# Ninth layer's attention in three-place steps with a written-out engine order, and the last layers' attention values by column strips

## The chip, the cores and the metric

The kernel runs on one core of one Trainium2 chip. The metric is the device time of one execution in microseconds (us); each kernel's time is the median of several runs. Engine names as the profile has them: PE (TensorE, matmuls), PEld (its weight loads), DVE (VectorE), ACT (ScalarE), POOL (GpSimd), SP (SyncE, which issues the transfers).

## The reference, cut to what matters

Twelve layers, four blocks of cross attention, attention and feed-forward, each added to `x` after a layer norm. `x` is 128 x 32 x 128 (batch, sequence, channels), all in float32. The change touches the ninth layer and the eleventh.

```
# ninth layer (L2_ffn): T, B, C = 128, 32, 128; H = 16 heads of D = 8
x0 = layernorm(x)
q, k, v = split(x0 @ in_proj_w.T + in_proj_b)             # attention runs over the 128 batch entries
attn = softmax(einsum('tbhd,sbhd->bhts', q, k) / sqrt(D))  # for each of 32 places b and 16 heads: 128 x 128
ctx  = einsum('bhts,sbhd->tbhd', attn, v)
h = layernorm(x0 + ctx @ out_w.T + out_b, ln1_g, ln1_b)
logits = h @ router_w.T + router_b                         # the router picks one of 8 experts, gelu, layernorm
# eleventh layer (L3_attn): 128 sequences of 32, 16 heads of 8
scores = einsum('bhqd,bhkd->bhqk', q, k) * scale + rel_bias
out = einsum('bhqk,bhkd->bhqd', softmax(scores), v) @ W_out.T + b_out
```

## The kernel before, in words

`x` lives on chip as eight tiles `X[g]` (128 rows x 4 x 128). The layers run one after the other, each in stages over groups; a tile framework puts each engine's instructions in an order at compile time, by the order in which the program writes them and by what they wait for. Tiles come from pools with a fixed number of buffers, and a new tile waits until the old user of its buffer is done. `issue_after(i)` keeps what is written inside it behind instruction `i` on its engine.

**Ninth layer, `L2_ffn`.** `x` goes through DRAM so that a row becomes a batch entry: `XB[q]`, eight groups `q` of four places. For a group: `stats` (DVE, with a power on POOL for the inverse root, L214), `normed` to `xn`, four transposes `pxt` copied by ACT to `xT`, projections `pq`, `pk`, `pv` to `QT`, `KT`, `V` by DVE. Then `L2_ffn_place` for each of the four places, and `end(q-1)`: second layer norm, transposes `pht`, `HT` (ACT), router `plg`, `LG` (DVE).

A place has two halves. `L2_ffn_scores`: POOL makes `KM` (the keys masked by head, L248); four score matmuls, one for each strip of 32 rows, fill four banks `S` (L1388, L1391; one buffer each); for each bank DVE takes the negated maximum `nm` (L1398, L1396) and ACT makes four exps with their sums `sm` (L1401). `L2_ffn_values`: sixteen transposes into banks `pt` of two buffers (L1412), copied to `ET` by DVE (L1417), the fourth by ACT (L1415); four matmuls `pav`, one for each strip of 32 output partitions (L1419, L1423); reciprocal of `sm` (L1424), spread by POOL to `rb` (L1426), transposed to `pr` (L1429), copied by ACT to `Rs` (L1431); DVE forms `O` = `pav` x `Rs` (L1433). `L2_ffn_out`: four matmuls `pw` (L1441), added to `xn` by DVE (L1442). All of `pxt`, `pq`, `pk`, `pv`, `pht`, `plg`, `pav`, `pr`, `pw` share a PSUM pool `bpq` of two buffers.

`L2_ffn_place` writes the scores of place n first, then the output of place n-2 and the values of place n-1, and orders PE alone: scores behind the `pr` of the values written before them, the rest behind the scores. Group work is written between the places, all of a group at once:

```
                    for i in range(4):
                        self.L2_ffn_place(QT[:, i, :], KT[:, i, :], V[:, i, :], xn[:, i, :], WO, st, ba, bps, bpt, bpq)
                    ends.append(lambda q=q, xn=xn: end(q, xn))
                    if q:
                        ends.pop(0)()
```

**Last layers, `L3`.** For each of eight groups the tenth layer (`xattn13`), the eleventh (`L3_attn`) and, one group later, the twelfth (`L3_ffn`) are interleaved by `abreast`. `L3_attn` works on 4 sets of four sequences per group, 32 in all: scores `S` of 32 x 32 blocks (L1528), bias and maximum (DVE), exp (ACT), 32 x 32 transposes on DVE to `ET`, values spread to `Vb` by POOL (L620). Then 16 value matmuls `po` (L1543) in two halves of eight heads, all with outputs on partitions 0 to 31; for each half a reciprocal (L1545) and a multiplication to `O` (L1546); four transposes `pot` (L1550), `OT` copied by ACT (L1552), one projection matmul `pw` (L1554), added to `X` by DVE (L1555). `po`, `pot` and `pw` share two buffers of `lpo`.

Of the kernel before, what the change touches and what calls it, by code (L numbers as in the profile page):

```python
# [9 lines left out]
FP = mybir.dt.float32  # L10
I32 = mybir.dt.int32
U32 = mybir.dt.uint32
AF = mybir.ActivationFunctionType
# [26 lines left out]
def _kxm(a):  # L40

    return np.ascontiguousarray(a.T)


def _blocks(d):
# [61 lines left out]
    f["L3_attn"] = [("wqkv", _kxm(g(p + "W_qkv"))), ("wo", _kxm(g(p + "W_out"))), ("bo", _rep(g(p + "b_out"))),  # L107
# [57 lines left out]
class Kern:  # L165
# [1099 lines left out]
    def L2_ffn(self, w):  # L1265
# [8 lines left out]
        with self.pool("bx") as bx:  # L1274
# [8 lines left out]
            with self.pool("bw") as bw, self.pool("bs", 2) as bs, self.pool("ba", 2) as ba, self.pool("bps", 1, PSUM) as bps, \  # L1283
# [3 lines left out]
                def end(q, xn):  # L1287
                    mv, rs = self.stats(bs, xn, 4, 1e-5)
                    h = Hn[q]
                    for i in range(4):  # L1290
                        nc.vector.tensor_scalar(h[:, i, :], xn[:, i, :], mv[:, i, 0:1], rs[:, i:i + 1], ALU.subtract, ALU.mult)
                    ps = bpq.tile([128, 512], FP, tag="q", name="pht")
# [3 lines left out]
                    nc.gpsimd.tensor_tensor(h, h, rep("b1n"), ALU.add)  # L1296
                    ps = bpq.tile([128, 4, 8], FP, tag="q", name="plg")
# [3 lines left out]
                st, ends = {}, []  # L1301
                for q in range(NG):
                    mv, rs = self.stats(bs, XB[q], 4, 1e-5)
                    xn = self.normed(bs, XB[q], mv, rs)
                    ps = bpq.tile([128, 512], FP, tag="q", name="pxt")
                    self.transposed(ps, xn)
                    nc.gpsimd.tensor_tensor(xn, xn, rep("bo"), ALU.add)
                    xT = bs.tile([128, 512], FP, tag="xT")
                    nc.scalar.copy(xT, ps)
                    QT = bs.tile([128, 4, 128], FP, tag="QT")  # L1310
                    ps = bpq.tile([128, 4, 128], FP, tag="q", name="pq")
                    nc.tensor.matmul(ps, lhsT=w["wi"][:, 0:128], rhs=xT, start=True, stop=True)
                    nc.vector.tensor_scalar(QT, ps, w["bqk"][:, 0:1], HD ** -0.5, ALU.add, ALU.mult)
                    KT = bs.tile([128, 4, 128], FP, tag="KT")
                    ps = bpq.tile([128, 4, 128], FP, tag="q", name="pk")
                    nc.tensor.matmul(ps, lhsT=w["wi"][:, 128:256], rhs=xT, start=True, stop=True)
                    nc.vector.tensor_scalar(KT, ps, w["bqk"][:, 1:2], None, ALU.add)
                    V = bs.tile([128, 4, 128], FP, tag="V")
                    ps = bpq.tile([128, 4, 128], FP, tag="q", name="pv")
                    for i in range(4):  # L1320
                        nc.tensor.matmul(ps[:, i, :], lhsT=xT[:, i * 128:(i + 1) * 128], rhs=w["wi"][:, 256:384], start=True, stop=True)
                    nc.vector.tensor_tensor(V, ps, rep("bv"), ALU.add)
                    for i in range(4):
                        self.L2_ffn_place(QT[:, i, :], KT[:, i, :], V[:, i, :], xn[:, i, :], WO, st, ba, bps, bpt, bpq)
                    ends.append(lambda q=q, xn=xn: end(q, xn))
                    if q:
                        ends.pop(0)()
                self.L2_ffn_place(None, None, None, None, WO, st, ba, bps, bpt, bpq)
                ends.pop(0)()
# [27 lines left out]
    def L2_ffn_place(self, qT, kT, v, acc, WO, st, ba, bps, bpt, bpq):  # L1357

        tc = self.tc
        last = None  # L1360
        if qT is not None:
            if "pr" in st:
                with tc.issue_after(st["pr"].ins):
                    E, sm, last = self.L2_ffn_scores(qT, kT, ba, bps)
            else:
                E, sm, last = self.L2_ffn_scores(qT, kT, ba, bps)
        with tc.issue_after(last.ins) if last is not None else ExitStack():
            if "out" in st:
                self.L2_ffn_out(*st.pop("out"), WO, bpq)
            if "val" in st:  # L1370
                Ep, smp, vp, accp = st.pop("val")
                O, st["pr"] = self.L2_ffn_values(Ep, smp, vp, ba, bpt, bpq)
                st["out"] = O, accp
        if qT is not None:
            st["val"] = E, sm, v, acc
        else:
            self.L2_ffn_out(*st.pop("out"), WO, bpq)

    def L2_ffn_scores(self, qT, kT, ba, bps):
# [3 lines left out]
        KM = ba.tile([128, 4, 128], FP, tag="KM")  # L1383
        self.masked4(nc.gpsimd, KM, kT)
        E = ba.tile([128, H, 128], FP, tag="E")
        sm = ba.tile([128, H], FP, tag="sm")
        S = [bps.tile([128, 4, 128], FP, tag=f"s{j}", name="S") for j in range(4)]
        last = nc.tensor.matmul(S[3], lhsT=qT[96:128], rhs=KM[96:128], start=True, stop=True)  # L1388
        with self.tc.issue_after(last.ins):
            for j in range(3):  # L1390
                last = nc.tensor.matmul(S[j], lhsT=qT[32 * j:32 * j + 32], rhs=KM[32 * j:32 * j + 32], start=True, stop=True)  # L1391
# [226 lines left out]
```

## Time and profile before

| | |
|---|---|
| median of 3 runs | 5587.87 us (5586.97 to 5591.53) |
| the profiled execution's own time | 5588.02 us |
| its span, first to last instruction | 5586.2 us |
| mean granted PE clock | 0.893 |
| busy: PE, PEld, DVE, ACT, POOL | 4724.7, 3187.2, 3465.5, 2210.5, 1084.1 us |

The profile is of one execution. Busy time is a share over the whole span; the stages have different limits, so the stage is read by its own window, and in it by what each engine waited for. The granted clock is full (1.0) or half (0.5) at any moment, and a window's figure is the mean. A matmul in float32 counts as two entries on PE, a transpose as one.

### The profile page before, as it was taken

What the parts mean: (1) busy time and instruction counts of PE and PEld (TensorE: products, weight loads), DVE (VectorE), ACT (ScalarE), POOL (GpSimd) and SP (SyncE); (2) the same over time, 40 slices, a digit from 0 to 9 for tenths busy, and PEclk for the clock granted to TensorE, in tenths of its full rate; (3) what the DMA queues carried; (4) which work ended last, traced back from release to release, by engine and by line L of the source; (5) the groups of instructions that cost most, each with busy time, mean ns of one, the idle gap of its engine ahead of it and who ended that gap; (6) DMA issues with size and microseconds to landing.
All of it is one profiled execution on the core that took longest, in us unless ns stands there. A gap on an engine that the chain in (4) does not pass through costs nothing. (4 is left out here: it accounts for less than half of the span.)

```text
span 5586.2 us, 89363 instructions
## 1 busy us (share of the span) xinstructions
PE 4724.7 (85%) x34462; PEld 3187.2 (57%) x34462; DVE 3465.5 (62%) x9687; ACT 2210.5 (40%) x5844; POOL 1084.1 (19%) x1065
## 2 busy tenths in 40 slices
PE   8999989898889988898995888888988856668677
PEld 5666656666566656666772555555555533336445
DVE  4333359743884389639724788888788745456554
ACT  3333334333333333355331444454445525453233
POOL 0010102020111111111000222223222221212443
PEclk9999999998899989898995899999999967779777
DMA  3111131123012311231100000100010010000100
GB/s 97 39 43 38 43 57 43 43 58 57 29 40 55 68 34 43 81 56 52 20 5 17 25 20 28 31 26 22 27 29 24 26 38 1 1 1 10 35 12 11
DMA packets 335131, 192.95 MB, mean 35 GB/s; under 512 B 160865, under 2 KB 317281, under 8 KB 334065
## 3 DMA queue, kind: packets, MB, share of 16 engines
q1 hardware_dynamic: 334706, 187.24, 12.7%
q8 instruction: 272, 4.46, 0.3%
q14 instruction: 153, 1.25, 0.1%
HBM read 156.23 MB, written 30.96 MB: 34 GB/s over the span
## 5 line engine op out<-in xcount | busy, mean ns | idle before, releaser
L494 PE MATMUL S<-cT,t 128*128 128x257 f32 x2048 | 552.0, 401 | 65.1 <-ACT E L498 64.3
L214 POOL TENSOR_TENSOR rs<-ve,w_const 128x4 f32<-128x4 f32 (+1 forms) x192 | 193.0, 1006 | 1810.6 <-DVE ve L212 1738.9
L494 PEld LDWEIGHTS S<-cT,t 128*128 128x128 f32 x2048 | 366.6, 194 | 192.0 <-ACT E L498 111.4
L496 DVE TENSOR_REDUCE nm<-S 128x1 f32<-128x257 f32 x512 | 214.7, 421 | 406.1 <-PE S L494 403.5
L498 ACT ACTIVATE E<-S,nm 128x257 f32<-128x257 f32 x512 | 243.4, 476 | 385.1 <-DVE nm L497 380.2
L760 DVE SCALAR_TENSOR_TENSOR X<-py,R,X 128x128 f32<-128x128 f32 x768 | 221.9, 342 | 251.6 <-PE py L753 161.9
L1092 PE MATMUL S<-cT,QM 128*128 128x289 f32 x1024 | 355.9, 445 | 22.5 <-ACT E L1094 20.4
L1094 ACT ACTIVATE E<-S,nm 128x289 f32<-128x289 f32 x512 | 254.9, 501 | 204.2 <-DVE nm L1093 201.7
L518 PE MATMUL po<-TA,cN 128*128 128x512 f32 x512 | 308.3, 690 | 13.0 <-ACT TA L513 12.6
L1101 PE MATMUL pt<-w_const,E 128*96 128x128 f32 (+1 forms) x1536 | 275.3, 291 | 45.7 <-ACT E L1094 38.3
L1101 PEld LDWEIGHTS pt<-w_const,E 128*96 128x96 f32 (+1 forms) x1536 | 190.3, 149 | 183.5 <-ACT E L1094 77.8
L520 ACT COPY OT<-po 128x512 f32<-128x512 f32 x256 | 150.0, 586 | 348.9 <-PE po L519 348.8
L519 PE MATMUL po<-TB,cN 128*128 128x512 f32 x512 | 284.1, 641 | 0.0
L753 PEld LDWEIGHTS py<-w_L_ffn,Hh 128*128 128x128 f32 x2048 | 251.2, 195 | 53.1 <-issue 32.7
L481 ACT COPY t<-pq 128x512 f32<-128x512 f32 x256 | 149.3, 586 | 325.7 <-PE pq L480 325.4
L480 PE MATMUL pq<-xT,WQK 128*128 128x128 f32 x2048 | 251.5, 279 | 27.4 <-DVE xn L220 16.6
L749 ACT ACTIVATE Hh<-pu,w_L_ffn 128x512 f32<-128x512 f32 x256 | 173.4, 687 | 228.7 <-PE pu L748 215.8
L753 PE MATMUL py<-w_L_ffn,Hh 128*128 128x128 f32 x2048 | 259.1, 280 | 3.7 <-ACT Hh L749 3.5
L480 PEld LDWEIGHTS pq<-xT,WQK 128*128 128x128 f32 x2048 | 238.9, 191 | 38.2 <-DVE xn L220 22.1
L1093 DVE TENSOR_REDUCE nm<-S 128x1 f32<-128x289 f32 x512 | 223.4, 449 | 57.2 <-PE S L1092 51.7
L748 PE MATMUL pu<-xT,w_L_ffn 128*128 128x512 f32 x512 | 250.4, 611 | 0.8 <-ACT Hh L749 0.8
L651 DVE TENSOR_TENSOR elt<-A,row 128x544 f32<-128x544 f32 (+23 forms) x304 | 246.8, 812 | 3.4
(477 smaller groups left out, 10775.0 us busy)
## 6 DMA issues: line engine op xcount, KB each, us to landing
cT<-ctxT SPq DMA_DIRECT2D x128, 257.0 KB
cN<-ctx SPq DMA_DIRECT2D x128, 256.0 KB
cT<-ctxT SPq DMA_DIRECT2D x32, 514.0 KB
phik<-PW SPq DMA_DIRECT2D x32, 256.0 KB
phiq<-P SPq DMA_DIRECT2D x32, 256.0 KB
A<-phik SPq DMA_DIRECT2D x64, 128.0 KB
PQ<-phiq SPq DMA_DIRECT2D x32, 256.0 KB
cN<-ctx SPq DMA_DIRECT2D x32, 194.0 KB
```

What stands on the lines that cost most here:

```text
L480: nc.tensor.matmul(ps[:, k, :, :], lhsT=WQK[:, 4 * j + k, cb * 128:(cb + 1) * 128], rhs=xt, start=True, stop=True)
L494: nc.tensor.matmul(S, lhsT=QP[j][:, cb, b, :, :], rhs=cTs[b][:, cb, :], start=cb == 0, stop=cb == 1)
L498: nc.scalar.activation(E[:, j, 0:LK], S, AF.Exp, bias=m, accum_out=sm[:, j:j + 1])
L518: nc.tensor.matmul(po, lhsT=cNs[b][:, 0, c], rhs=TA, start=True, stop=False)
L519: nc.tensor.matmul(po, lhsT=cNs[b][:, 1, c], rhs=TB, start=False, stop=True)
L651: nc.vector.tensor_tensor(t, A[:, k, :, i0:i1].rearrange("p h i -> p i h").unsqueeze(3).to_broadcast([128, m, HC, n]), row[:, :, i0:N].uns ...
L748: nc.tensor.matmul(ps, lhsT=wu[:, e, k * 128:(k + 1) * 128], rhs=xT[:, q, :], start=True, stop=True)
L753: nc.tensor.matmul(py[:, i, :], lhsT=Hh[:, k, i * 128:(i + 1) * 128], rhs=wd[:, e, k, :], start=k == 0, stop=k == 3)
L1092: nc.tensor.matmul(S, lhsT=QM[:, 0, 4 * j:4 * j + 4, :], rhs=cT[:, b, :], start=True, stop=True)
L1093: nc.vector.tensor_reduce(nm[:, j:j + 1], S, AX.X, ALU.max, negate=True)
L1094: nc.scalar.activation(E[:, j, :], S, AF.Exp, bias=nm[:, j:j + 1], accum_out=sm[:, j, b:b + 1])
L1101: nc.tensor.transpose(pt[0:n, j * 128:(j + 1) * 128], E[:, j, k0:k1], self.ident)
```

## The change

In `L2_ffn` the function `L2_ffn_step(n, ...)` takes the place of `L2_ffn_place`, `_scores`, `_values` and `_out`. A step works on three places: scores of n, values of n-1, output of n-2. Helper `follow` chains each listed instruction behind the one listed before it on its engine, so that PE, DVE and ACT each have the order of the text; POOL's work and the group's work on DVE and ACT are not chained. The first three of a place's four transpose banks are made in its own step, the fourth in the next; ACT now copies the third bank, DVE the others. The group's work becomes two generators, `front(q)` and `end(q)`, of which a step takes one piece each; their PE instructions are chained in at that point. Keys are projected ahead of queries, `xn` has three buffers, `sm` three.

In `L3_attn` the value matmuls put head `4j+k` on output partitions 32j to 32j+31, in one bank; one reciprocal and one multiplication follow; four transposes have 128 input partitions and 32 output partitions, ACT copies 32 x 512 for 128 x 128, and the projection is four matmuls over 32 rows each, with `wo` laid out as 32 x 512.

```diff
-    f["L3_attn"] = [("wqkv", _kxm(g(p + "W_qkv"))), ("wo", _kxm(g(p + "W_out"))), ("bo", _rep(g(p + "b_out"))),
+    f["L3_attn"] = [("wqkv", _kxm(g(p + "W_qkv"))), ("bo", _rep(g(p + "b_out"))),
+                    ("wo", g(p + "W_out").T.reshape(4, 32, 128).transpose(1, 0, 2).reshape(32, -1)),
...
+                def front(q):
+                    mv, rs = self.stats(bs, XB[q], 4, 1e-5)
...
+                    nc.scalar.copy(xT, ps)
+                    yield 1
...
+                    nc.vector.tensor_scalar(KT, ps, w["bqk"][:, 1:2], None, ALU.add)
...
+                    nc.vector.tensor_scalar(QT, ps, w["bqk"][:, 0:1], HD ** -0.5, ALU.add, ALU.mult)
+                    yield 1
...
+                    nc.vector.tensor_tensor(V, ps, rep("bv"), ALU.add)
+                    P[q] = QT, KT, V, xn
+                    yield 1
+                def end(q):
+                    xn = P.pop(q)[3]
                     mv, rs = self.stats(bs, xn, 4, 1e-5)
...
+                    yield 1
                     ps = bpq.tile([128, 512], FP, tag="q", name="pht")
...
+                    yield 1
                     ps = bpq.tile([128, 4, 8], FP, tag="q", name="plg")
...
+                for n in range(T + 2):
+                    q, i = n // 4, n % 4
...
+                    if i == 0 and q + 1 < NG:
+                        new = front(q + 1)
+                    old = end(q - 1) if i == 1 and q else old
+                    self.L2_ffn_step(n, pl, ((new,), (new, old), (new, old), (old,))[i], WO, st, ba, bps, bpt, bpq)
...
+    def queue(self, st, *insts):
+        for i in insts:
+            if i.engine in st:
+                self.tc.add_manual_dep(i, st[i.engine].name, mybir.DependencyInfo(mybir.DependencyClass.NoSync, mybir.DependencyReason.DATA),
+                                       reason="issue_after")
+            st[i.engine] = i
...
+    def L2_ffn_step(self, n, pl, side, WO, st, ba, bps, bpt, bpq):
...
+        a, b = st.get(n - 2), st.get(n - 1)
+        if a:
+            a["Rs"] = ba.tile([128, 4, 128], FP, tag="Rs", name="Rs")
+            f(nc.scalar.copy(a["Rs"], a["R"]))
+        if pl is not None:
...
+            for j in (3, 0, 1, 2):
+                r = slice(32 * j, 32 * j + 32)
+                f(nc.tensor.matmul(S[j], lhsT=qT[r], rhs=KM[r], start=True, stop=True))
+        if b:
+            b["pt"] = b["p2"], transposes(b["E"], 3)
+            evacuated(b["ET"], nc.scalar.copy, b["pt"][0])
+        if a:
+            a["O"] = ba.tile([128, 4, 128], FP, tag="O", name="O")
+            f(nc.vector.tensor_tensor(a["O"], a["po"], a["Rs"], ALU.mult))
+        def maximum(j):
             nm = ba.tile([128, 4], FP, tag=f"nm{j}", name="nm")
+            f(nc.vector.tensor_reduce(nm, S[j], AX.X, ALU.max, negate=True))
             for k in range(4):
                 h = 4 * j + k
+                f(nc.scalar.activation(c["E"][:, h, :], S[j][:, k, :], AF.Exp, bias=nm[:, k:k + 1], accum_out=c["sm"][:, h:h + 1]))
+        if pl is not None:
+            maximum(0)
+        if b:
+            evacuated(b["ET"], nc.vector.tensor_copy, b["pt"][1])
+            f(nc.vector.reciprocal(b["sm"], b["sm"]))
...
+        if pl is not None:
+            maximum(1)
+        if a:
...
+                f(nc.tensor.matmul(pw, lhsT=a["O"][:, k, :], rhs=WO[:, k, :], start=k == 0, stop=k == 3))
+            f(nc.vector.tensor_tensor(a["acc"], a["acc"], pw, ALU.add))
...
+        for gen in side:
+            next(gen, None)
+        self.queue(st, *[i for i in traced[at:] if i.engine == nc.tensor.engine])
+        if pl is not None:
+            maximum(2)
+            p0 = transposes(c["E"], 0)
+            maximum(3)
+        if b:
...
+                f(nc.tensor.matmul(b["po"][r], lhsT=b["v"][:, r], rhs=b["ET"][j], start=True, stop=True))
...
+                f(nc.tensor.transpose(b["R"][:, k, :], rb[:, k].rearrange("p j c -> p (j c)"), self.ident))
+        if pl is not None:
+            evacuated(c["ET"], nc.vector.tensor_copy, p0)
+            evacuated(c["ET"], nc.vector.tensor_copy, transposes(c["E"], 1))
+            c["p2"] = transposes(c["E"], 2)
...
+            ps = lpo.tile([128, 4, 4, HD + 1], FP, tag="o", name="po")
+            for k in range(4):
+                for j in range(4):
+                    h = 4 * j + k
+                    nc.tensor.matmul(ps[32 * j:32 * j + 32, k], lhsT=ET[:, h, :], rhs=Vb[:, h], start=True, stop=True)
+            nm = lt.tile([128, 4, 4], FP, tag="nm")
+            nc.vector.reciprocal(nm, ps[:, :, :, HD])
...
+            pt = lpo.tile([32, 4, 4, T], FP, tag="o", name="pot")
             for b in range(4):
+                nc.tensor.transpose(pt[:, b].rearrange("p j q -> p (j q)"), O[:, b].rearrange("p k d -> p (k d)"), self.ident)
+            OT = lt.tile([32, 4, 4, T], FP, tag="OT")
+            nc.scalar.copy(OT, pt.rearrange("p b j q -> p j b q"))
             pw = lpo.tile([128, 128], FP, tag="o", name="pw")
+            for j in range(4):
+                nc.tensor.matmul(pw, lhsT=OT[:, j].rearrange("p b q -> p (b q)"), rhs=wo4[:, j, :], start=j == 0, stop=j == 3)
             nc.vector.tensor_tensor(self.X[g][:, i, :], self.X[g][:, i, :], pw, ALU.add)
             yield 1
```

## The prediction

> **What bounds the kernel now.** I read the page first, for the span and the clock, then the busy time of two stretches: the ninth layer's attention (its first score matmul at 4593.6 us to the router at 5045.5) and the last three layers (from 5230).
>
> ```profile
> span 5586.2 us, 89363 instructions
> ...
> PEclk9999999998899989898995899999999967779777
> ```
> ```profile
> 4593.60:5045.50 451.90, 310.63 (x1610) 172.16 (x1610) 223.32 (x527) 227.97 (x1104) 88.19 (x97) 0.76 0.00 1
> ...
> 5230.00:5586.20 356.20, 278.13 (x2799) 181.80 (x2797) 176.05 (x626) 115.87 (x227) 141.28 (x132) 0.74 0.04 12
> ```
>
> After the bounds and the length come the busy us of PE, weight load, DVE, ACT and POOL, then the granted clock. In the attention no engine is full: PE 69%, DVE 49%, ACT 50%, at a clock of 0.76. So it is a chain. The timeline of one place shows it:
>
> ```profile
> 4818.07 0.69 PE L1388 MATMUL S<-KM,QT 32*128 32x512 f32 x1 [1.08 <-POOL KM L248]
> ...
> 4819.24 0.69 DVE L1398 TENSOR_REDUCE nm<-S 128x4 f32<-128x512 f32 x1 [1.52 <-PE S L1391]
> ...
> 4820.03 0.37 ACT L1401 ACTIVATE E<-S,nm 128x128 f32<-128x128 f32 x1 [7.64 <-DVE nm L1398]
> ...
> 4825.53 0.68 ACT L1415 COPY ET<-pt 128x512 f32<-128x512 f32 x1
> ...
> 4826.26 1.06 PE L1419 MATMUL pav<-ET,V 128*32 128x512 f32 x1 [2.43 <-ACT ET L1415]
> ...
> 4828.12 1.12 PE L1429 MATMUL pr<-w_const,rb 128*128 128x128 f32 x4
> ...
> 4829.17 0.84 PE L1388 MATMUL S<-KM,QT 32*128 32x512 f32 x1
> ```
>
> The loop S, maximum, 16 exps (5.50 us), ET, pav, pr, next S is 11.10 us long, and its links take turns: the values of the place before stand in line behind the exps of this one (the ET copy is ACT's seventeenth), and PE waits 2.43 us. The 31 distances from first S (4593.61) to last S (5024.77) average 13.91 us; four are 55.6, of which 4 x 11.1 = 44.4 are places and 11.2 is group work (stats, projections, router) in which the places stand still.
>
> In the last layers PE is 78% busy, and the lines that the change touches are
>
> ```profile
> L1543 PE MATMUL po<-Vb,ET 128*32 128x36 f32 x1024 | 53.0, 224 | 23.7 <-DVE ET L1538 20.9 <-DVE mv L197 2.8
> ...
> L1554 PE MATMUL pw<-w_L_attn,OT 128*128 128x128 f32 x64 | 18.4, 377 | 6.5 <-ACT OT L1552 6.5
> L1550 PE MATMUL pot<-w_const,O 32*128 32x32 f32 x128 | 15.7, 249 | 13.9 <-DVE O L1546 13.9
> ```
>
> The chain of waits puts 12.8% of these 356.2 us on po (45.6 us), 3.8% on pw, 3.6% on pot, 2.8% on O.
>
> **A plain step, summed from rows.** It is counted from the last exp of one place to that of the next, at full clock. S must wait for that exp (each score bank has one buffer); S and its hand-over take 1.2 (4818.07 to 4819.24). Beside it ACT copies Rs (0.59) and DVE forms O (0.69), queued ahead of the first maximum: 1.4 with hand-overs, so O sets the time. Maximum 0.69, hand-over 0.1, exps 5.50, the last accumulator read 0.2. DVE has an ET copy (0.68), the reciprocal (0.25) and the second maximum (0.68) = 1.61 to do while ACT does four exps (1.37): 0.24 more. Sum 1.4 + 0.69 + 0.1 + 5.5 + 0.24 + 0.2 = 8.1 us. ET, pav and pr have left the loop: PE does them while ACT does exps.
>
> Do the engines fit in 8.1? PE at full clock: S and pav 2 entries each at 0.45 (4833.92 to 4834.37), 20 transposes and 8 entries of pw at 0.105 (8 in 1.04 less 0.2 of drain): 1.8 + 2.1 + 0.84 = 4.7; a group adds pxt, pht, pq, pk, pv, plg = 4.3, a quarter of it per step: 5.8 at full clock, 11.6 at half. DVE: O 0.69, four maxima and three copies 4.76, reciprocal 0.25, sum 0.28 = 6.0, and 8.4 per group = 8.1. ACT 7.0 + 0.34. At full clock PE is covered; DVE just is.
>
> **What the group work costs in its steps**, in the compiled order of each engine. Step 0: xT (0.59) stands among the exps. Step 1: QT, KT and one stat (1.78) stand ahead of the fourth maximum, which had 1.1 to spare: 0.7. Step 2 is the dear one: end's h (1.12, behind a POOL power of 1.02) and the next front's power (1.02) are queued on DVE ahead of O and of the first maximum; that maximum is 2.3 late, the rest of xn delays the second by another 0.9, and HT (0.78) stands among the exps: 4.0. PE waits then too: pht's bank is free only after the sum that follows the second maximum, some 3 us of idle. Step 3: 0.2. A group: 4 x 8.13 + 0.6 + 0.7 + 4.0 + 0.2 = 38.0.
>
> **The clock.** In the timeline's stretch 4821.4 to 4824.8 PE was busy 1.25 of 3.4 us at clock 1.00; the next 3.4 us were granted 0.69. Idle like that of step 2 is thus followed by half clock. A stretch at half clock costs up to 1.7 us of PE; I take one and a half per group, 2.6, between 0 (hidden behind exps) and 9 (a rival, below). Group 40.6, step 10.15. The Trainium skill ("TensorE: Matmul & The Clock Gate", Part 1) says that the clock halves after an idle window of about 3.4 us; by a wholly idle window none of these gaps would count, and the group would be 38.0. The trace disagrees: 2.43 us of idle (4823.8 to 4826.3) was enough.
>
> The gain is 31 x (13.91 - 10.15) = 116.6 us. Fill and drain keep their length: two more steps run without scores, as the last values and outputs did.
>
> **The last layers, per place** (32), at full and half clock. po, 32 entries in one column strip, takes 1.23 (5432.47) or 2.10 (5418.40). Over four strips there is no row; the nearest is pav, whose four strips ran together (8 entries of 512 in 1.93, two serial ones being 1.7). So 8 rounds of 0.04 or 0.065 plus 0.2: 0.5 or 0.75, against 1.23 or 2.10 if the strips did not overlap. pot: 4 x 0.105 + 0.2 = 0.63 for 0.40 (half clock 1.05 for 0.63). pw: 8 entries for 2, 1.05 for 0.49 (1.9 for 0.80). OT has 512 columns for 128: 0.59 (as Rs) for 0.27. DVE behind the last po: 0.25 + 0.28 (rows of the reciprocal and of the sum) for 0.34 + 0.41. Sum +0.16 or +0.27 per place, 5 to 9 us if all is on the chain. DVE loses 64 x 0.74 - 32 x 0.53 = 30 us of busy time, which is a gain wherever DVE ends a wait: -20 at best. If po does not overlap it is +28 or more. I take +5, range -20 to +28. The weight block of the eleventh layer grows by 197 KB; it is issued at 4495.8 and first read after 5220: nothing. The first transfers (4577 to 4583) stay.
>
> **Sum.** 5588.02 - 116.6 + 5 = 5476.4 us, against the profiled execution's own 5588.02, which is 0.15 over the median of 5587.87.
>
> **Rivals.** (1) *Half clock throughout.* PE idles about 2.3 us in a plain step; if that never lets the clock rise, PE needs 11.6 per step and some 0.7 of drains: 12.3, gain 31 x 1.6 = 50, last layers +9: 5547. For it: the present 0.76. Against: at half clock PE would be full, and full stretches are granted 1.00 (4818.0 to 4821.4, busy 3.10 of 3.4). Counted over the whole trace in stretches of 3.41 us at full clock: with transposes busy 0.3 to 0.5 and other matmuls 0.2 to 0.4 of a stretch, the clock stayed up in 16 of 19; with the same other matmuls and under 0.15 of transposes, in 3 of 36. The Trainium skill (the same page, Part 4) says that transposes do not count as busy for the clock; 20 matmuls of a step are such, and by that rule this rival would be the forecast. The count speaks against it.
> (2) *DVE and POOL let the work flow better*: no half clock, step 9.3, last layers -15: 5588 - 143 - 15 = 5430.
> (3) *Slower: the fixed order closes the ring again.* The third transpose bank needs the first ET copy, which DVE does behind the fourth maximum; S is queued behind it. If group work holds that maximum back in every step, places go in turn: 11.1 + 2.8 of group work + a power and h on DVE (3.2 / 4) = 14.7 per step, +25 us, and +9: 5622. It decides from 13.91 per step. Against: in plain steps the copy ends 1.3 us before the last exps.
> (4) *The order does not come out*: but the compiled program has it; only its cover could fail, which is (1).
>
> **How the numbers follow.** Forecast 0.60, (1) 0.19, (2) 0.11, (3) 0.08, (4) or nothing 0.02. The range reaches from the group of 38.0 with -20 below (5588 - 137 - 15, 5436) to most of (1): 5436 to 5545. A measurement here tells 0.2%, 11 us, from no change: faster 0.90, same 0.02, slower 0.08.
>
> **What would show it.** Right: distances of first S near 10.2 with one long step in four; PE's wait for the ACT copy of ET ahead of pav (73.1 us) gone; exps waiting on maxima instead; clock of the stretch over 0.76; po of 32 entries under 0.8 us, pw about doubled, the last stretch within 30 us of 356. Wrong: a step over 12, a clock under 0.7, or a last stretch above 390.

## The result, and the profile after

The changed kernel takes **5422.23 us** (median of 4 runs, 5418.07 to 5425.24), the kernel before 5587.42 (4 runs): ratio 0.9705, 95% interval 0.9688 to 0.9721. That is 165 us where the prediction had 112, and below its range. One execution of number 8 below ran in a slower state (6706.44 us at a mean clock of 0.635) and is left out, so its median is of three. The page of the profiled execution:

```profile
span 5423.5 us, 89730 instructions
...
PEclk9999989999899989988998699999899996899777
```

The slices in which the ninth layer lies, the 35th to 37th, show an 8 and two 9s; they were three 7s, the 34th to 36th, before. By stage, from the traces of the two kernels (first score matmul to first score matmul; us of the span):

| stretch | before | changed | difference | forecast |
|---|---|---|---|---|
| start to the ninth layer's first score | 4593.6 | 4606.5 | +12.8 | 0 |
| first to last score, 31 steps | 431.2 | 279.9 | -151.3 | -116.6 |
| last score to the last layers' first | 210.0 | 205.9 | -4.1 | 0 |
| last layers | 351.4 | 331.3 | -20.1 | +5 |
| span | 5586.2 | 5423.5 | -162.7 | -111.6 |

The first row is unchanged code; over the traces below it lies between 4579.4 and 4606.5, so these 13 us are not put down to the change. The windows of the second and fourth row (bounds, length, busy us of PE, weight load, DVE, ACT, POOL, then the granted clock):

```profile
4606.45:4886.30 279.85, 237.43 (x1522) 141.23 (x1521) 211.15 (x492) 215.16 (x1066) 84.17 (x94) 0.92 0.00 1
5092.21:5423.50 331.29, 274.11 (x2980) 175.04 (x2980) 154.63 (x555) 119.80 (x222) 138.81 (x130) 0.75 0.04 12
```

In the ninth layer ACT and DVE do the same work as before and are now busy 77% and 75% of it, at a clock of 0.92 for 0.75. In the last layers PE's busy time is what it was (274.9 before), and DVE has 20 us less. First a plain step, then the long one, from the timeline of the changed kernel:

```profile
4854.47 0.69 ACT L1405 COPY Rs<-pr 128x512 f32<-128x512 f32 x1
4854.73 1.14 PE L1415 MATMUL S<-KM,QT 32*128 32x512 f32 x8 [1.06 <-ACT E L1427]
...
4855.19 0.69 DVE L1421 TENSOR_TENSOR O<-pav,Rs 128x512 f32<-128x512 f32 x1 [1.36 <-ACT Rs L1405]
...
4855.91 0.69 DVE L1424 TENSOR_REDUCE nm<-S 128x4 f32<-128x512 f32 x1
...
4856.72 0.37 ACT L1427 ACTIVATE E<-S,nm 128x128 f32<-128x128 f32 x1 [1.07 <-DVE nm L1424]
...
4862.46 1.14 PE L1415 MATMUL S<-KM,QT 32*128 32x512 f32 x8 [1.06 <-ACT E L1427]
```
```profile
4733.38 1.11 DVE L1321 TENSOR_SCALAR Hn<-xn,mv,rs 128x128 f32<-128x128 f32 x4 [0.27 <-POOL rs L215]
4734.41 0.68 DVE L1421 TENSOR_TENSOR O<-pav,Rs 128x512 f32<-128x512 f32 x1
...
4736.29 1.06 DVE L1293 TENSOR_SCALAR xn<-XB,mv,rs 128x128 f32<-128x128 f32 x1 [1.12 <-POOL rs L215]
4737.27 0.68 DVE L1424 TENSOR_REDUCE nm<-S 128x4 f32<-128x512 f32 x1
...
4738.06 0.37 ACT L1427 ACTIVATE E<-S,nm 128x128 f32<-128x128 f32 x1 [4.06 <-DVE nm L1424]
...
4740.26 0.66 PE L228 MATMUL pht<-w_const,Hn 128*128 128x128 f32 x4 [3.06 <-DVE xn L1441]
```

The plain step runs as it was summed: Rs and S, then O, the first maximum, exps; from one first S to the next it takes 7.72 us. The long one shows what the prediction called the dear step: h, POOL's power and xn stand ahead of the first maximum, ACT waits 4.06 us and PE 3.06. The groups of instructions that answer to those of before, with their waits:

```profile
L1427 ACT ACTIVATE E<-S,nm 128x128 f32<-128x128 f32 x512 | 180.1, 395 | 73.1 <-DVE nm L1424 73.1
L1456 PE MATMUL pav<-ET,V 128*32 128x512 f32 x256 | 38.4, 676 | 0.5
...
L1565 PE MATMUL po<-Vb,ET 128*32 128x36 f32 x1024 | 17.8, 221 | 23.8 <-DVE ET L1560 16.9 <-DVE mv L198 6.5
L1572 PE MATMUL pot<-w_const,O 128*32 128x128 f32 x128 | 26.8, 349 | 5.3 <-DVE O L1569 5.2
L1577 PE MATMUL pw<-w_L_attn,OT 32*128 32x128 f32 x256 | 48.3, 342 | 6.8 <-ACT OT L1574 6.1
```

`pav` waits 0.5 us in all, where ACT's copy held it for 73.1. `po` fell from 53.0 to 17.8 us, `pot` and `pw` rose from 34.1 to 75.1 together.

### The profile page after: what moved, and what is told of

It is laid out like the page before. It is cut to its first block, busy times and chain, and to the rows that moved or that the text cites. A ratio compares the mean times of both kernels' runs of the same rounds, so it can differ in the third digit from the quotient of the medians.

```text
span 5423.5 us, 89730 instructions
## 1 busy us (share of the span) xinstructions
PE 4669.2 (86%) x34654; PEld 3162.2 (58%) x34654; DVE 3445.6 (64%) x9623; ACT 2212.1 (41%) x5844; POOL 1082.4 (20%) x1065
## 5 line engine op out<-in xcount | busy, mean ns | idle before, releaser
L519 PE MATMUL po<-TA,cN 128*128 128x512 f32 x512 | 312.8, 699 | 13.0 <-ACT TA L514 12.6
L754 PEld LDWEIGHTS py<-w_L_ffn,Hh 128*128 128x128 f32 x2048 | 253.9, 197 | 52.9 <-issue 32.6
L530 PE MATMUL pout<-WVO,OT 128*128 128x128 f32 x2048 | 243.1, 277 | 6.2 <-ACT OT L521 6.2
```

The source lines that it names most:

```text
L519: nc.tensor.matmul(po, lhsT=cNs[b][:, 0, c], rhs=TA, start=True, stop=False)
L530: nc.tensor.matmul(po[:, 0, :], lhsT=OT[:, cb, h, :, :], rhs=WVO[:, cb, h, :], start=h == 0 and cb == 0, stop=False)
L754: nc.tensor.matmul(py[:, i, :], lhsT=Hh[:, k, i * 128:(i + 1) * 128], rhs=wd[:, e, k, :], start=k == 0, stop=k == 3)
```

## The experiments

All times are set against the kernel before, run on the same chip. Since the unchanged code ahead of the ninth layer differs by up to 27 us between traces, effects of 5 to 20 us are read from the stage windows, one trace for each run.

**1 and 2. Each half of the change alone.** One kernel has the new ninth layer and the old last layers, the other the reverse (`wo` goes with the last layers):

```diff
 # 1: as changed, but in L3_attn, with wo as before
-            ps = lpo.tile([128, 4, 4, HD + 1], FP, tag="o", name="po")
+            for q in range(2):
+                ps = lpo.tile([32, 8, 4, HD + 1], FP, tag="o", name="po")
...
 # 2: as before, but in L3_attn, with wo as changed
-            for q in range(2):
-                ps = lpo.tile([32, 8, 4, HD + 1], FP, tag="o", name="po")
+            ps = lpo.tile([128, 4, 4, HD + 1], FP, tag="o", name="po")
...
```

> Only the ninth layer's attention is changed; the last layers compute their values as before. Theory A (the ledger of the two traces: the ninth layer gave some 155 us, the last layers 20): about 5440 us, first score to last score about 280 us, last stretch (first score of the tenth to twelfth layers to the end) about 351 us. Rival B (the last layers became faster because of something upstream, not by their own edit): the last stretch is 331 here too and the time is that of the whole change, 5422.

> Only the values of the last layers are changed; the ninth layer stays as before. Theory A (the edit itself is worth 20 us): about 5567 us, last stretch about 331 us. The prediction's term (+5): about 5592, last stretch about 356. Rival B (the gain came from upstream): last stretch 351, 5587.

Ninth alone: 5425.74 us, ratio 0.9716 (0.9703 to 0.9729). Last layers alone: 5574.91, 0.9981 (0.9971 to 0.9991), that is -10.6 us (-16 to -5). The windows of the first:

```profile
4583.89:4856.35 272.46, 227.10 (x1530) 135.62 (x1530) 212.20 (x493) 214.78 (x1067) 85.01 (x94) 0.96 0.00 1
5061.45:5408.12 346.67, 272.13 (x2788) 178.05 (x2788) 174.53 (x619) 112.79 (x222) 138.97 (x130) 0.75 0.04 12
```

The last stretch is 333.6 us with the new values (second kernel) and 346.7 with the old, so by the windows theory A holds: the gain comes with the edit to these layers, not from upstream. By its time number 1 lies nearer to B's 5422 than to A's 5440, because its ninth layer is 8 us and its last stretch 4 us shorter than A took them; and number 2 gains 10.6 us by its time where A had 20. Over all traces the new values, unaltered, took 327.7 to 337.0 us (eight traces, mean 332.4), the old ones 346.7 and 351.4: 17 us, where single traces of the same code differ by up to 9. And there is a thing that neither theory had: the ninth layer takes 272.5 us here, to the end of its last score, at a clock of 0.96, and 281.0 at 0.92 in the changed kernel, with the same instructions in the same order.

**3 and 4. Last layers: strips in turn; division in halves.**

```diff
-            for k in range(4):
-                for j in range(4):
+            for j in range(4):
+                for k in range(4):
                     h = 4 * j + k
                     nc.tensor.matmul(ps[32 * j:32 * j + 32, k], ...)
```
```diff
-            nc.vector.reciprocal(nm, ps[:, :, :, HD])
-            nc.vector.tensor_tensor(O..., ps[:, :, :, 0:HD], nm..., ALU.mult)
+            for z in range(2):
+                y = slice(2 * z, 2 * z + 2)
+                nc.vector.reciprocal(nm, ps[:, y, :, HD])
+                nc.vector.tensor_tensor(O[:, :, y]..., ps[:, y, :, 0:HD], nm..., ALU.mult)
```

> The whole change, but the 16 matmuls of po go through the four column strips one after the other (j outside, k inside), so that consecutive matmuls share a strip. Theory C (the last layers gain because po over four strips overlaps: 54.3 to 17.8 us of PE): po costs 1.2 to 2.1 us per place again, 32 x 0.7 to 1.5 = 23 to 48 us more PE time on the chain, last stretch 350 to 375, time 5440 to 5465. Theory D (they gain because DVE has 20 us less to do): last stretch 331 to 340, time 5422 to 5430.

> The whole change, but the reciprocal and the multiplication of O are done in two halves each, as before: DVE has 64 + 64 instructions again, some 0.3 us more per place, 10 us busy in all. Theory D (DVE's relief is the gain): last stretch 10 to 15 us longer, time 5432 to 5437. Theory C (overlap of po): 0 to 4 us longer, 5422 to 5426.

Strips in turn: 5416.05 us, 0.9703 (0.9690 to 0.9717), last stretch 337.2. `po` rose to 33.4 us of busy PE from 17.8, so the overlap of the strips is real; but only 5 of these 16 us reach the stretch, at the edge of what unaltered code varies. The range of C, 350 to 375, is missed; the stretch lies in D's, 331 to 340. Halves: 5406.86, 0.9681 (0.9667 to 0.9695), last stretch 329.5. By their own rows the halves cost 13.8 + 12.6 us for 9.0 + 8.1, so 9 us more, as expected; DVE's busy time in the stretch is 154.5 us all the same, since other rows are shorter and some overlap. The 10 to 15 us of D do not show; but the edit brings back only 9 of the 30 us of these rows (25.0 + 21.9 before), and none of the total.

**5 and 6. Ninth layer: group work all at once; only PE's order fixed.**

```diff
         for gen in side:
-            next(gen, None)
+            for _ in gen:
+                pass
```
```diff
-            if i.engine in st:
+            if i.engine in st and i.engine == self.nc.tensor.engine:
                 self.tc.add_manual_dep(...)
```

> The whole change, but the group work isn't spread: the next group's whole front in step 0, the whole end of the group before in step 1. Theory E (spreading is worth little, since most of the gain is the values that left the ring): PE stands in line behind stats, xn, xT, KT and QT in one step, 3 to 6 us per group more than the 37.6 us of a spread group, 8 groups: 5446 to 5470 us. Rival F (spreading is what removes the 11.2 us of group work): 11 us per group, 5500 us or more.

> The whole change, but only PE's order is fixed; DVE's and ACT's is left to the scheduler, which puts the first ET copy and the sum behind all four maxima and O in the same place. Theory G (PE's order carries the gain; exps need nothing but their maximum): within 10 us of 5422. Rival H (the order on DVE and ACT matters): the ET copy is 2 us later, the values are late for the next step: 1 to 2 us per step, 5450 to 5480.

All at once: 5454.64 us, 0.9777 (0.9750 to 0.9805), and

```profile
4592.42:4911.47 319.05, 249.81 (x1538) 149.56 (x1538) 219.92 (x494) 217.31 (x1067) 84.24 (x94) 0.90 0.00 1
```

319 us for 281: spreading is worth 38 us, 5 per group, as E had it (5455 us in its 5446 to 5470); the steps with group work are 10.9 and 15 us long, the other two of a group 7.72. The larger part, some 114 of the 152 us by which 433.3 became 281.0, is put down to the values having left the ring of links that take turns: plain steps are 7.72 us here too, where a place took 11.1. With only PE's order fixed: 5404.09, 0.9683 (0.9661 to 0.9705), ninth layer 272.5. H falls, and the written order on DVE and ACT adds nothing that shows here; the time is 18 us under the changed kernel's, more than the 10 that G allowed, of which 8.5 lie in the ninth layer.

**7, 8 and 12. Ninth layer: three other places for the work.** The first puts stats a step ahead of their normalisation and chains the group's DVE and ACT work behind the sum. The second, on top of it, takes the heads in the order 3, 0, 1, 2 and makes three scores and two maxima of the next place early. The third leaves the group's ACT work and most of its DVE work to the scheduler, but chains xn and h on DVE behind a step's last ET copy:

```diff
 # 7: front() and end() yield behind stats; front(q + 2) starts in step 3
+                    yield 1
...
-        self.queue(st, *[i for i in traced[at:] if i.engine == nc.tensor.engine])
+        self.queue(st, *[i for i in traced[at:] if i.engine in (nc.tensor.engine, nc.vector.engine, nc.scalar.engine)])
```
```diff
 # 8: at the end of step n, with heads in the order 3, 0, 1, 2
+            p0 = transposes(c["E"], 0)
+            score(n + 1, 0)
+            evacuated(c, 0, nc.vector.tensor_copy, p0)
+            maximum(n + 1, 3)
+            c["p2"] = transposes(c["E"], 1)
+            score(n + 1, 1)
+            maximum(n + 1, 0)
```
```diff
 # 12: the yields of 7, and at the end of a step
+        at = len(traced)
+        for gen in late:          # xn of the next group in step 0, h of the last in step 1
+            next(gen, None)
+        self.queue(st, *[i for i in traced[at:] if i.engine == nc.vector.engine])
```

> A better place for the group work: the stats (with POOL's power) one step ahead of the normalisation that needs them, and the group work's DVE and ACT instructions in the fixed order behind the sum, not ahead of O and the first maximum. Theory I (the dear step of 12.3 us is h, power and xn ahead of O and the first maximum): it falls to 9 or less, a group to 34 to 35 us, 7 groups x 3 = 20 us less: about 5400. Rival J (the clock or PE's own length sets it): no change, 5415 to 5425.

> As the one with the fixed group work, and the heads go in the order 3, 0, 1, 2, so that three of the four scores and two of the maxima of the next place are done while ACT still does the exps of this one. Theory K (in a plain step ACT idles some 2.4 us between the last exp and the next first exp for S, O and the first maximum): ACT has 7.1 us and DVE 8.0 of work per step, so a step is about 8.1 us, 31 x (9.03 - 8.1) = 29 us less: about 5393. Rival L (PE's fixed order closes the ring again, since a score waits for a free bank in front of the values): 9 us per step or more, 5420 or above.

> The ninth layer's group work in other places of the steps: the stats of the next group one step ahead of its normalisation, xn and h on DVE behind the last ET copy of a step (where DVE waits 1.1 to 2.0 us for Rs), transposes, projections and router on PE as before. Theory R (the long step of 10.7 to 11.3 us is h and xn in one gap ahead of O and the first maximum): it falls to 8.5 to 9, a group of four from 35.6 to 33.5, the ninth layer to about 258 us, time 13 to 16 us under the changed kernel. Rival S (DVE is the bound: 6.0 + 2.0 us per step): group 35 or more, no change.

The first is slower than the change, 5438.08 us, 0.9740 (0.9715 to 0.9765), with a ninth layer of 304.6 at 0.85. Its timeline, the end of a row of eight stats between the second and the third maximum:

```profile
4749.79 0.45 DVE L213 TENSOR_SCALAR ve<-mv 128x4 f32<-128x4 f32 x1
4750.16 1.27 DVE L1429 TENSOR_REDUCE nm<-S 128x4 f32<-128x512 f32 x2
...
4750.87 0.37 ACT L1432 ACTIVATE E<-S,nm 128x128 f32<-128x128 f32 x1 [2.18 <-DVE nm L1429]
...
4752.17 0.41 PE L1401 MATMUL pt<-w_const,E 128*128 128x128 f32 x2 [1.85 <-DVE ET L1405]
```

The third maximum is late, exps wait 2.18 us, the ET copies behind it are late too and PE waits 1.85. Theory I missed, and so did J: the longest step still takes 11.5 us (12.3 in the change), and the other steps of a group rose to between 8.7 and 10.9. The edit moved the delay to other maxima: a mild form of the mechanism of rival (3). The second gave 5405.76, 0.9690 (0.9661 to 0.9719), ninth layer 273.8: 31 us less than the first, on which it is built, and 8.8 us per step, between K's 8.1 and L's 9. What K wanted of plain steps did not come: they stay at 7.7 us, since ACT now waits for PE:

```profile
4845.47 0.59 ACT L1400 COPY ET<-pt 128x512 f32<-128x512 f32 x1 [1.43 <-PE pt L1396]
```

The third is 5393.26, 0.9656 (0.9640 to 0.9673), beside 5418.29 for the changed kernel (number 9):

```profile
4598.89:4852.79 253.90, 228.91 (x1530) 137.54 (x1530) 210.43 (x499) 214.76 (x1067) 84.08 (x93) 0.96 0.00 1
```

The long step fell to 8.4 (sometimes 9.5), the group from 37.6 to 32.1 (33.2 with the longer step): R holds, and S falls, since DVE is 83% busy and not the bound. Of the 27 us between 281.0 and 253.9, 19 are the placing, by the 272.5 us of the old placing at the same clock of 0.96 (number 1); the rest goes with the clock.

**9. The changed kernel once more.**

> The changed kernel itself once more, beside the next three. In the kernels run so far with the same ninth layer it took 272.5 to 273.0 us at a granted clock of 0.96, in the changed kernel's own profile 281.0 at 0.92. Theory M (the clock at which this stretch runs differs between executions of one program): time between 5405 and 5425 us, the ninth layer 273 or 281. Rival N (it is a property of the program): 281 and 0.92 again, 5418 to 5425.

5418.29 us, 0.9705 (0.9688 to 0.9722), ninth layer 281.0 at 0.92 again, N's numbers. This program has the longer of the two lengths in both its traces; why, is taken up below, and it does not have to be the program. 281.0 or 280.9 came in three traces (two of this program, one of number 11), 278 in two, 272.4 to 273.2 in six, all with the same ninth layer, each engine's instructions in the same order.

**10. DVE's load put back, off the chain.** Behind the true `O`:

```diff
+            for z in range(2):
+                nc.vector.reciprocal(nm2, ps[:, :, :, HD])
+                nc.vector.tensor_tensor(O2..., ps[:, :, :, 0:HD], nm2..., ALU.mult)
```

> The whole change, and in the last layers DVE repeats the reciprocal and the multiplication of O twice into tiles that nobody reads, behind the true ones: DVE has 32 x 2 x 0.53 = 34 us more to do, a little over what the change took from it; the chain from po to pw is as long as in the change. Theory D (DVE's relief is the gain of the last layers, through the queue of DVE in which stats, E and ET stand): the last stretch goes back to 345 to 350 us, time 15 to 18 us over the changed kernel. Theory C' (PE's chain and the buffers are the gain): 331 to 335, 0 to 4 us over.

5411.28 us, 0.9695 (0.9677 to 0.9713), its ninth layer being 273.2. The last stretch:

```profile
5070.17:5409.50 339.33, 273.01 (x2980) 178.19 (x2980) 175.31 (x683) 120.22 (x222) 138.89 (x130) 0.73 0.04 12
```

DVE has its 175 us back and the stretch is 7 over the mean of 332.4: between the two theories, under half of the gain. PE's wait of `po` for ET is 34.1 us here, for 16.9, which fits D: ET stands in DVE's queue. The 339.3 are 2 us beyond the longest of the unaltered traces (337.0).

**13, 14, 16 and 17. The other parts put back.** Two `po` tiles, each with its own division (13); with that, DVE's work twice ahead of `pot` and strips in turn (14); strips in turn with each matmul of `po` issued twice (16); number 14 with each issued twice (17):

```diff
-            ps = lpo.tile([128, 4, 4, HD + 1], FP, tag="o", name="po")
+            for z in range(2):                             # 13, 14, 17
+                ps = lpo.tile([128, 2, 4, HD + 1], FP, tag="o", name="po")
...
+                for o in ("O2", None):                     # 14, 17: once into O2, then into O
+                    nc.vector.reciprocal(nm, ps[:, :, :, HD])
+                    nc.vector.tensor_tensor(to..., ps[:, :, :, 0:HD], nm..., ALU.mult)
...
+                    for _ in range(2):                     # 16, 17
                         nc.tensor.matmul(ps[32 * j:32 * j + 32, k], ...)
```

> The whole change, but po is two tiles of two head columns each, with a reciprocal and a multiplication for each, so that four tiles per place go through the two banks of their pool, as before the change (po, po, pot, pw), for three. Theory T (the number of passes through the two banks is what the DVE load left open): the last stretch 339 to 345 us. Theory U (it is the time from po to pw and DVE's load alone): 331 to 336.

> As the one before, and the strips go in turn, and each reciprocal and multiplication is done once more ahead of the true one, so that DVE has some 0.8 us of work behind each po, as before the change (0.74). Everything that the change took from po and DVE is back, and what it added to pot, OT and pw stays. If the gain of the last layers is made of these parts alone: last stretch 346 us or more, over the 347 to 351 of the old values by up to 9 (the price of pot, OT and pw): 346 to 360. If it comes from pot, OT and pw after all: 331 to 340.

> The whole change, with the strips in turn and every matmul of po issued twice (the second writes the same result), so that eight in a row share a strip, as before the change. PE's time in po comes back (53 us of busy, from 17.8), nothing else does. Theory V (PE's length in po is the larger part of the gain): last stretch 340 to 350 us. Theory W (PE's length in po is hidden behind what else bounds the stretch): 331 to 337.

> As the run with everything on the chain (two po tiles, DVE's work twice ahead of pot, strips in turn), and every matmul of po issued twice as well. Now PE's 30 us in po are back too, which that run had not brought back (22 us of busy against 53). If the gain is made of po's length, DVE's work and the tiles: 347 us or more. If pot, OT and pw have a part in it: 340 to 345.

| | us | ratio (interval) | last stretch | clock there |
|---|---|---|---|---|
| 13 two tiles | 5421.97 | 0.9725 (0.9708 to 0.9741) | 339.8 | 0.75 |
| 14 with DVE and strips | 5420.91 | 0.9726 (0.9709 to 0.9742) | 341.6 | 0.72 |
| 16 `po` twice | 5437.29 | 0.9723 (0.9692 to 0.9754) | 361.5 | 0.84 |
| 17 all of it | 5401.81 | 0.9673 (0.9640 to 0.9706) | 334.5 | 0.82 |

```profile
5073.98:5415.54 341.56, 299.20 (x2980) 182.59 (x2980) 172.95 (x747) 122.10 (x222) 138.83 (x130) 0.72 0.04 12
```
```profile
5078.17:5439.69 361.52, 308.83 (x4004) 214.90 (x4004) 150.17 (x555) 121.28 (x222) 139.43 (x130) 0.84 0.04 12
```
```profile
5067.88:5402.39 334.51, 298.37 (x4004) 204.78 (x4004) 173.33 (x747) 121.16 (x222) 138.84 (x130) 0.82 0.05 13
```

Two tiles cost 7 us, near the low end of T. Number 14 costs 9, between its two ranges and less than DVE's load and the two tiles one by one, and it lacked one part: its `po` took 22.2 us of PE, not 53. With `po` long and nothing else put back (16; 73.7 us of `po`, more than before the change) the stretch is 29 us longer: V's sign, beyond its range. But with all put back (17) it is 334.5, below both ranges of its expectation and among the unaltered traces, though 512 matmuls more than in 14. The clock, 0.82 for 0.72, lets these cost no more of PE's time than 14 took; it does not explain 16, which has 0.84 and is 27 us longer than 17, 17 of them idle PE (52.7 us for 36.1). The parts do not add. By 17's own expectation, a stretch under 345 says that `pot`, `OT` and `pw`, the parts that the prediction priced as a cost, have a share in the gain; no run isolates them.

One thing that none of these edits holds fixed is the compiled order. The framework orders each engine's instructions anew for every program. Of ACT's 221 instructions in the last stretch, on which numbers 4, 10, 13, 14, 16 and 17 change nothing, 8 to 74 stand in another place of the order than in the changed kernel; in number 3 and in all traces of the unaltered new values none does, and between the kernel before and the changed one 41 do. What that can do is seen in what was PE's longest wait before the change, that of the transposes `pxt` for the normalised `xn` (total us, times, longest; before, changed, number 13):

```profile
PE pxt L227 <- ACT xn L1489: 22.2, 13, 4.8
```
```profile
PE pxt L228 <- ACT xn L1510: 6.0, 5, 3.0
```
```profile
PE pxt L228 <- ACT xn L1510: 21.0, 10, 3.0
```

In four groups of the kernel before (six in number 13), ACT makes the `xn` of two layers, eight in a row, before it copies the first `xT` out of `pxt`; in the changed kernel the copy stands between the two (first before, the last five of eight, then changed):

```profile
5351.09 2.04 ACT L1489 ACTIVATE xn<-X,nb,rs 128x128 f32<-128x128 f32 x5 [0.51 <-DVE nb L1486]
5353.31 0.59 ACT L1585 COPY xT<-pxt 128x512 f32<-128x512 f32 x1 [0.18 <-PE pxt L227]
```
```profile
5203.67 0.58 ACT L1526 COPY xT<-pxt 128x512 f32<-128x512 f32 x1 [0.57 <-PE pxt L228]
5205.53 1.65 ACT L1510 ACTIVATE xn<-X,nb,rs 128x128 f32<-128x128 f32 x4 [1.27 <-DVE nb L1507]
```

In the three traces with eight in a row (before, 1 and 13) the wait is 20.7 to 22.2 us, in all others 3.5 to 10.1. So number 13 meets T's number, but brought this order back too, and T's mechanism, the passes through the two banks, is not shown by it.

**11 and 15. A better version.** In the last layers one transpose of 128 x 128 for four, and the projection in 16 matmuls of 32 x 32 over diagonal tiles, with `wo` four times on the partitions (11); with the third placement of the group work (15).

```diff
-            for b in range(4):
-                nc.tensor.transpose(pt[:, b]..., O[:, b]..., self.ident)
+            nc.tensor.transpose(pt..., O.rearrange("p b k d -> p (b k d)"), self.ident)
...
+                for b in range(4):
+                    r = slice(32 * b, 32 * b + 32)
+                    nc.tensor.matmul(pw[r], lhsT=OT[r, j, :], rhs=wo4[r, j, :], start=j == 0, stop=j == 3)
```

> The last layers' values by column tiles, but pot is one transpose of 128 x 128 per place (b, k, d on the partitions) for four, OT has 128 columns for 512, and pw is 16 matmuls of 32 x 32 over four diagonal tiles, with W_out four times on the partitions. Theory P (PE is 83% busy in the last stretch and its length counts): pot 26.8 to about 8 us of PE, pw 48 to 25..50, OT 0.30 us shorter per place on the way to pw; last stretch 315 to 322 us, time 10 to 15 us under the changed kernel. Theory Q (the four diagonal tiles do not overlap and pw takes 2 us per place): 331 or above.

> The two better versions together: group work in other places of the steps, and one transpose with diagonal tiles in the last layers. The stages are apart, so the gains add: ninth layer 254 us, last stretch 311 to 314, time 5360 to 5375, 0.960 of the kernel before. If the clock falls in one of them because of the other: 5375 to 5390.

Number 11: 5386.18 us, 0.9648 (0.9627 to 0.9669). Its groups and last stretch:

```profile
L1578 PE MATMUL pw<-w_L_attn,OT 32*32 32x128 f32 x1024 | 41.3, 307 | 2.4 <-ACT OT L1573 2.0
...
L1571 PE MATMUL pot<-w_const,O 128*128 128x128 f32 x32 | 10.3, 322 | 8.2 <-DVE ve L213 5.2 <-DVE O L1569 3.0
```
```profile
5071.47:5382.89 311.42, 258.56 (x3652) 152.89 (x3652) 154.73 (x555) 111.76 (x222) 138.87 (x130) 0.79 0.05 13
```

P holds, and more: four times the matmuls of `pw` took less PE time (41.3 us for 48.3, though one lasts 307 ns and there are 1024), so the diagonal tiles overlap. PE's busy time fell by 16 of the 21 us, at a clock of 0.79 for 0.75; the order of this stretch changed here as well. Both together: **5365.28 us** (5350.68 to 5365.66), as expected, 0.9606 (0.9591 to 0.9622), 1.0% under the changed kernel's 0.9705.

```profile
4595.89:4848.97 253.08, 228.34 (x1530) 137.46 (x1530) 210.38 (x499) 214.26 (x1067) 84.02 (x93) 0.96 0.00 1
5053.85:5363.85 310.00, 258.52 (x3652) 153.37 (x3652) 153.85 (x555) 111.71 (x222) 138.91 (x130) 0.79 0.05 14
```

The two gains add, stage by stage.

## Why the prediction was wrong

**Right:** the direction, the chain that held the ninth layer, what leaves it (the ET copy ahead of `pav`), what comes in its place (exps wait on the maxima, 73.1 us), the dear step (12.1 summed, 12.3 between first scores, with 3 us of idle PE). That a full group took 37.6 us where 38.0 was the sum at full clock is in part luck: at the clock of 0.96 it takes 35.6 to 36.1.

**The sum over 31 steps, 34.8 us too long.** The forecast of 314.7 is 31 plain steps (252.0), group work (5.5 per group, 42.6) and the clock (2.6 per group, 20.2). Measured 279.9, in three misses of like size:
- *The plain step* is 7.72 us, not 8.13: 31 x 0.41 = 12.7. The 0.24 added for DVE behind the first four exps and the 0.2 of the last accumulator read do not show: the 16 exps follow one another in 5.6 us, and ACT's next work begins while the last accumulator read runs. DVE's load was summed too high as well: 211.15 us of busy time are 6.8 us per step, not 8.1.
- *Group work taken for 31 equal steps.* In the kernel with a ninth layer of 271.3 (first to last score) all beyond 31 x 7.72 is 32.0, against 42.6. A full group there is 35.6 to 36.1, so 4.7 to 5.2 beyond its plain steps, near the 5.5; the rest is that the first group has no `end` and the last two carry little (their steps are 7.72 to 9.1 in the changed kernel's trace too). "31 x" was the wrong factor.
- *The clock.* 281.0 against 272.5 us for the same instructions is 8.5, not 20.2. In the changed kernel 46.0 us of the layer ran at half clock, in the other 19.9: 0.33 us of time per us of half clock, not the 0.5 that I took; that part of PE's slower work lies behind exps would explain it. The 271.3 still hold those 19.9 us at half clock, so some of the 32.0 is clock as well, and the split between the last two misses is rough.

The long step's 3.06 us of idle is followed by a window at half clock, from 4741.24 for 3.41 us, as 2.43 us were before. By the Trainium skill ("TensorE: Matmul & The Clock Gate", Part 1) it takes an idle window of about 3.4 us; 3.06 was enough here. The same part says that the window runs free, so that the phase at which work meets it differs from run to run; the traces agree. In all of them the clock changes on a grid of 3.41 us. Where the layer's first score came 1.6 to 1.9 us ahead of the next line of that grid (five traces; in the changed kernel 4606.45 and 4608.12), the layer took 278 to 281 us; where it came 2.7 to 3.2 us ahead (six traces; in number 1, 4583.89 and 4586.68), 272.4 to 273.2. In the traces of 281 the windows at half clock then come 20.5 and 17.1 us apart by turns, 37.5 in sum, as long as a group of 37.6, so every group meets the grid alike. No run set the phase, and number 6, with another order on DVE and ACT, took 272.5 us at 1.55; so this is read from traces and not tested.

**The last layers, +5 forecast, -17 measured** (-20.1 in the two traces, -10.6, with an interval of -16 to -5, for that half alone). The parts were sized well: `po` 0.47 and 0.71 us for 0.5 and 0.75, `pot` 0.60 and 1.04 for 0.63 and 1.05, `pw` 1.15 for 1.05 at full clock and 2.07 for 1.9 at half. The step that failed is the last one, "5 to 9 us if all is on the chain", with DVE's relief (its rows fell by the 30 us summed, its busy time by 20) as no more than a bound. It adds up the links of one place from `po` to `pw` and takes their sum for the time, in a stretch where PE stood idle for 76 us. PE's busy time did come out about even (274.9 to 274.1); what fell was that idle, to 57 us: `pxt` for `xn` from 22.2 to 6.0 us, `pot` for `O` from 13.9 to 5.2. The larger of the two goes with the order that the framework compiled for ACT, for which the prediction had no term. The cause of the 17 us stays open beyond that. DVE's load put back costs 7 us and a second `po` tile 7, each in one trace, 2 to 3 us beyond the longest unaltered one, and each with another compiled order; strips in turn, with the same order, cost 5, which unaltered code varies by too. How these share the 17, and whether `pot`, `OT` and `pw` help by themselves, is not settled.

**The rivals.** (2), "no half clock, step 9.3, last layers -15", with 0.11, was nearest: step 9.03, last layers -17, 5422 for 5430. The clock is not quite full, so its numbers fit better than its reason. (1), half clock throughout, fell: 0.92, and 0.98 in number 8. By the Trainium skill (the same page, Part 4) transposes do not count as busy for the clock; in number 8, as in the change, 20 of the 32 matmuls of a plain step are such, and it ran 276 us on end at full clock. The prediction's count depends on how stretches are cut: taken on the clock's own grid, full windows were followed by a full one in 18 of 26 cases with many transposes (it had 16 of 19) and in 1 of 31 with few (3 of 36), which says the same and speaks against that rule here. (3) did not occur in the change, but number 7 has a mild form of its mechanism, at 9.8 us per step. The chance of 0.11 for (2) was too low: two of its three parts were my own terms with smaller prices.

**The other rows.** "Fill and drain keep their length": -4.1. The +12.8 ahead of the layer came from code that was not touched.

## What to carry to other kernels

A chain of engines that take turns is shortened by letting each work on another place, and PE's order alone did it here; group work then belongs where its engine waits anyway, and moving it behind one maximum instead of another only moves the delay. In a sum over repeated steps count the first and the last groups separately, and where the bound is idle time of an in-order engine, price what it waits for, not its busy time. Where a framework compiles the order, compare the order of the untouched instructions before and after an edit, or a put-back tests two things at once. Cut PE's own length with tiles that run side by side: one transpose and diagonal tiles gave 21 us on top of the 17 that came with the strips.

## What the runs showed of the hardware

- One layer, with each engine's instructions in the same order, took 272.4 to 273.2 us (six traces) or 278 to 281 (five): the granted clock changes on a grid of 3.41 us, and the two lengths go with the place of the layer's first score on that grid (2.7 to 3.2, or 1.6 to 1.9 us ahead of its next line).
- With every matmul of `po` issued twice, strip after strip, the last stretch took 29 us more (361.5 us for 332.4), although the clock there was 0.84 for 0.75. Beside the DVE work and the second tile the same 512 matmuls made it no longer: 341.6 us at a clock of 0.72 without and 334.5 at 0.82 with them, one trace each, 7 us apart where unaltered code varies by 9.
- A reciprocal and a multiplication on DVE over half the columns took 197 and 216 ns for 252 and 280: two halves cost 26.4 us where the whole cost 17.1.
